# Layer 1's values by whole tiles of tokens, and four residual sums moved to TensorE, in a four-layer graph network on one core

## The chip, the cores and the metric

The kernel runs on one core of a Trainium2 chip. The metric is device time in microseconds (us), from the first to the last work of one execution; lower is better. The core has five engines that run side by side: TensorE (PE in the profile, with its weight loads as PEld), VectorE (DVE), ScalarE (ACT), GpSimd (POOL) and SyncE (SP), which issues the DMAs. In this kernel TensorE writes its results to PSUM, and VectorE and ScalarE bring them from there to SBUF.

## The reference

The input x has 128 graphs of 64 nodes with 256 features, all in FP32, and one 64 x 64 weighted adjacency matrix that all graphs share. Four layers follow, each with a residual and a layer norm around it:

```
x = layernorm(x + gnn0(x))   # A_hat x -> 512 -> batch norm, relu -> 256 -> batch norm
x = layernorm(x + gnn1(x))   # Chebyshev step, 4-head masked attention, MLP
x = layernorm(x + gnn2(x))   # two graph convolutions, then LSTMs over windows of 1..4 nodes
x = layernorm(x + gnn3(x))   # graph attention
```

Two places matter here. Layer 0 ends with a batch norm of its output over all tokens, whose scale and shift are known only when all tokens have been seen; then comes `x + out` and its layer norm. In layer 1 the attention needs queries, keys and values of the same tokens:

```
q, k, v = x1 @ Wq, x1 @ Wk, x1 @ Wv        # 4 heads of 64
o = softmax(mask(q k^T / 8)) v             # within each graph of 64 nodes
```

## The kernel before

The 8192 tokens are cut into 16 blocks of 512 (`TB`), which is 8 graphs. A block is held in SBUF either token-major (`tm`: 128 tokens in the partitions, four tiles of 256 features, `NT` = 4) or feature-major (`fm`: 128 features in the partitions, two chunks of 512 tokens). One such buffer is 128 x 1024 FP32. A token tile of 128 holds two graphs, one in each half of the partitions (`halves`).

Buffers come from two stocks. `PS` has four PSUM tiles of 128 x 1024; `mem` has SBUF tiles of the same shape. A step takes a tile, and the step that empties it gives it back.

The order of instructions on the engines is written by a planner, `flow`, while the program is built. Each task (one block of one layer, one LSTM unit, one load) is a generator. Before each group of instructions it yields `step(engine, us, ...)`: the engine, the planned duration, how many PSUM and SBUF tiles it takes, whether later steps of the task wait for it, and a label `tbl` that stands for an activation table on ScalarE or for the way TensorE's array is divided. A change of that label on TensorE is charged 0.1 us. At each turn `flow` takes the step that can begin soonest, after adding a margin that is multiplied by a pseudo-random factor; the numbers in `DRAWS`, one for each 50 us of planned time, choose these factors. So `DRAWS` decides the order of everything from the end of layer 0 on, but adds no work. Each engine executes its list in order and waits at semaphores for its inputs.

Where the plan leaves TensorE without work, `keep_awake` issues filler products of the identity (L142). Their number comes from the planned gap less 0.4 us, divided by 0.86 us.

Layer 0 runs as `first_block` and `second_block` for the 16 blocks; then `bn_coeffs` gives the batch norm's scale `sc2` and shift `sh2`. After that, one call of `flow` plans the end of layer 0 and layers 1 to 3 together. Its streams are the ends of layer 0 and the blocks of layer 1 (`seq`, up to six at a time), the graph convolutions of layer 2 (`gcn_block`), its LSTM units and the blocks of layer 3 (`last_block`).

`end_block(i)` ends layer 0 for one block. It loads x again from HBM (L771), applies scale and shift on ScalarE (L774, feature-major), transposes to token-major with 8 transposes of 128 x 128 (`to_tm`, L376), and adds x on VectorE out of PSUM (L782, one instruction of 128 x 1024). Block 0 (`NORMED`) is also normalised there; for the others `block` begins with that layer norm. A layer norm takes statistics on VectorE (L302 to L304), a power on GpSimd (L325), a small product on VectorE (L328) and four activations on ScalarE (L331). The blocks are not ended in their own order:

```
ends = (0, 1, 12, 13, 14, 15, 2, 3, 8, 9, 10, 11, 4, 5, 6, 7)
at_end = {0: 4, 1: 4, 2: 8, 3: 10, 4: 14, 5: 16}
```

so blocks 0, 1, 12 and 13 are ended before layer 1 begins block 0, and 14, 15, 2 and 3 before it begins block 2.

`block(i)` is layer 1 for one block: the norm, an aggregation with the graph's matrix in quarters of the array (L358), a product with Wc by whole token tiles (`mm_tm`, L394), an addition and a norm, the transposes to feature-major (`to_fm`, L370), the products with Wq and Wk (`mm_fm`, L382), the values (L846), the scores in quarters of the array (L872), the softmax, transposes of its result (L905), the product with the values in quarters (L919), Wo by `mm_tm`, and the MLP.

The values are computed graph by graph. For each of the 8 graphs and each half r of the heads, the stationary operand is 64 tokens of x1 (64 columns) and the moving one 128 columns of Wv; half r of the heads goes to half r of the PSUM partitions. So two products run in the two column halves of the array, and the PSUM tile has the layout that L919 wants: a whole-tile copy on ScalarE (L856) brings it to SBUF.

Of the kernel before, what the change touches and what calls it, by code (L numbers as in the profile page):

```python
# [11 lines left out]
ALU = mybir.AluOpType  # L12
# [3 lines left out]
P = 128  # L16
B, N, D = 128, 64, 256
NBLK = 16
TB = 512
NT = 4  # L20
# [8 lines left out]
LAG, LAG_T = 0.06, 0.2  # L29
MARGIN = {"T": 0.5, "V": 0.5, "S": 0.5}  # L30
STRETCH = 50.0
DRAWS = [119, 456, 684, 0, 152, 590, 97, 0, 0, 316, 775, 750, 291, 668, 396, 690, 972, 316, 700, 299, 810, 345, 289, 861, 902, 463, 567, 883, 455, 277, 848, 910, 108, 288, 531, 607, 103, 756, 415, 205, 829, 978, 419, 437, 870, 596, 976, 248, 270, 919]


@with_exitstack
def kernel(ctx: ExitStack, tc: tile.TileContext, a: dict, out: bass.AP):
    nc = tc.nc
    V, S, G, T = nc.vector, nc.scalar, nc.gpsimd, nc.tensor
# [11 lines left out]
    def tm(s):  # L50

        return s.rearrange("p (t d) -> p t d", t=NT)

    def fm(s):

        return s.rearrange("p (c k) -> p c k", c=2)
# [60 lines left out]
    def mark(*key):  # L117
        done[key] = Clock.end
# [7 lines left out]
    def step(e, us, ps=0, sl=0, waits=True, at=None, tbl=None):  # L126

        return (e, us, ps, sl, waits, at, tbl)
# [9 lines left out]
    def flow(streams, margin, start=0.0):  # L144
# [8 lines left out]
        def drawn(k, t):  # L153

            j = int(t / STRETCH)
            d = DRAWS[j] if j < len(DRAWS) else 0
            return (k * 7919 + j * 104729 + d * 1299709) * 2654435761 % 4294967296 / 2147483648 if d else 1.0
# [84 lines left out]
    def ctile(shape, name, pool=cp):  # L242
        return pool.tile(shape, F32, tag=name, name=name)
# [4 lines left out]
    Xs = [Xp[i // 2][:, i % 2, :] for i in range(NBLK)]  # L248
# [3 lines left out]
    H = [fm(s) for s in Hs]  # L252
# [3 lines left out]
    PS = Stock([ctile([P, NT * D], f"ps{j}", psp) for j in range(4)])  # L256
    mem = Stock([ctile([P, NT * D], f"t{j}", big) for j in range(TEMPS)])
# [15 lines left out]
    halves = slice(0, N), slice(N, P)  # L273
    for s in range(2):
        h = halves[s]
# [8 lines left out]
    ident = ctile([P, P], "ident")  # L284
# [34 lines left out]
    def ln_steps_act(y):  # L319

        n = y.shape[1]
        yield step("V", 0.3 + 0.53 * n)
        mv, rs = stats(y)
        yield step("G", 1.0)
        G.tensor_tensor(rs, rs, neghalf[:, :n], ALU.pow)  # L325
        yield step("V", 0.2, tbl="m")
        nm = sm.tile([P, n], F32, tag="ln_nm", name="ln_nm")
        V.scalar_tensor_tensor(nm, mv[:, :, 0], -1.0, rs, ALU.mult, ALU.mult)  # L328
        yield step("S", 0.1 + 0.5 * n)
        for t in range(n):  # L330
            S.activation(  # L331
                y[:, t, :], y[:, t, :], AF.Identity, scale=rs[:, t : t + 1], bias=nm[:, t : t + 1]
            )
# [38 lines left out]
    def to_tm(ps, yT):  # L372

        for t in range(ps.shape[1]):
            for c in range(2):
                T.transpose(ps[:, t, c * P : (c + 1) * P], yT[:, c, t * P : (t + 1) * P], ident)  # L376
# [13 lines left out]
    def mm_tm(ps, yT, w, nk):  # L390

        for t in range(NT):
            for k in range(nk):
                T.matmul(  # L394
                    ps[:, t, :],
                    yT[:, k, t * P : (t + 1) * P],
                    w[:, k, :],
                    start=(k == 0),
                    stop=(k == nk - 1),
                )  # L400
# [22 lines left out]
    with c0:  # L423
# [310 lines left out]
        Wc, Wq, Wk, Wv = (WA[:, j, :].rearrange("p (k m) -> p k m", k=2) for j in range(4))  # L734
# [24 lines left out]
    sc2, sh2, _ = bn["bn2"]  # L759

    Wv_par = Wv.rearrange("p k (u r e) -> p k r u e", u=2, r=2)

    NORMED = range(1)

    def end_block(i):
        x = X[i]
        yield step("Q", 6.0, sl=1)
        xin = mem.take()  # L770
        nc.sync.dma_start(tm(mem[xin]), x_blk[i])  # L771
        for c in range(2):
            yield step("S", 0.7)
            S.activation(  # L774
                H[i][:, c, :], H[i][:, c, :], AF.Identity, scale=sc2[:, c : c + 1], bias=sh2[:, c : c + 1]
            )
        yield step("T", 0.9, ps=1)
        ps = PS.take()
        to_tm(tm(PS[ps]), H[i])
        mark("h", i)  # L780
        yield step("V", 1.25, ps=-1)
        V.tensor_tensor(x, tm(PS[ps]), tm(mem[xin]), ALU.add)  # L782
        PS.give(ps)
        mem.give(xin)
        if i in NORMED:
            yield from ln_steps_act(x)
        mark("end", i)

    def block(i):
        x = X[i]  # L790
        mark("begun", i)
        if i not in NORMED:
            yield from ln_steps_act(x)
        yield step("T", 0.98, ps=1, sl=1, tbl="quarter")
        ps = PS.take()
# [6 lines left out]
        ps = PS.take()  # L802
# [14 lines left out]
        ps = PS.take()  # L817
        s_x1 = mem.take()
        to_fm(fm(PS[ps]), y)
        yield step("S", 1.05, ps=-1)  # L820
        x1T = fm(mem[s_x1])
# [3 lines left out]
        for w in (Wq, Wk):  # L825
            yield step("T", 3.45, ps=1, sl=1)
            ps = PS.take()
# [8 lines left out]
        qT, kT = fm(mem[qk[0]]), fm(mem[qk[1]])  # L836


        yield step("T", 3.6, ps=1, sl=1, tbl="columns")
        ps = PS.take()  # L840
        s_v = mem.take()
        pv = PS[ps].rearrange("p (b u e) -> p b u e", b=8, u=2)
        for b in range(8):
            for r in range(2):
                for k in range(2):
                    T.matmul(  # L846
                        pv[r * N : (r + 1) * N, b, :, :],
                        x1T[:, k, b * N : (b + 1) * N],
                        Wv_par[:, k, r, :, :],
                        start=(k == 0),  # L850
                        stop=(k == 1),
                    )
        mem.give(s_x1)
        yield step("S", 1.05, ps=-1, waits=False)
        v = mem[s_v].rearrange("p (b u e) -> p b u e", b=8, u=2)
        S.copy(mem[s_v], PS[ps])  # L856
        PS.give(ps)

        yield step("G", 2.4, waits=False, tbl="m")
# [4 lines left out]
        ps = PS.take()  # L864
        s_e = mem.take()
        pq = PS[ps].rearrange("p (r g m) -> p r g m", r=2, g=8)
        for t in range(NT):
            for u in range(2):
                for s in range(2):
                    b = 2 * t + s  # L870
                    for r in range(2):
# [4 lines left out]
                            start=True,  # L876
                            stop=True,
# [4 lines left out]
        e = mem[s_e].rearrange("p (g r m) -> p g r m", g=8, r=2)  # L882
# [19 lines left out]
        ps = PS.take()  # L902
# [9 lines left out]
        ps = PS.take()  # L912
        s_o = mem.take()
        po = fm(PS[ps])
        for b in range(8):
            t, s = b // 2, b % 2
            for u in range(2):
                for r in range(2):
# [4 lines left out]
                        start=True,  # L923
                        stop=True,
# [7 lines left out]
        ps = PS.take()  # L932
# [9 lines left out]
        ps = PS.take()  # L942
# [13 lines left out]
        for hf in range(2):  # L956
            yield step("T", 3.45, ps=1, sl=1)
            ps = PS.take()
# [14 lines left out]
        ps = PS.take()  # L973
        for t in range(NT):
            for k in range(4):
# [4 lines left out]
                    start=(k == 0),  # L980
                    stop=(k == 3),
# [487 lines left out]
    def sum_weights(p, sums):  # L1469
# [18 lines left out]
        for k in range(2):  # L1488
            i0, i1, h0, h1 = (w[:, k, :, c, :] for w in (ih, hh) for c in range(2))
            s1, s2, s3, s4 = (gates(sums[2 * i + k]) for i in range(4))  # L1490
            for dst, y, z, op in (
# [8 lines left out]
                else:  # L1500
                    for g in range(4):
                        V.tensor_tensor(S4[k][g], y[:, g], z[:, g], op)
        WS[p] = {
            "A11": block(ih, 0), "A12": block(hh, 0), "A22": block(hh, 1),
            "S1": whole(S1), "S2": whole(S2), "S3": whole(S3), "S4": whole(S4),
        }
# [136 lines left out]
    for i in blocks:  # L1643
        while n < at_end.get(i, NBLK):
            j = ends[n]
            seq.append((None, lambda j=j: end_block(j), 1))
            n += 1
        seq.append((lambda i=i: ready(("end", i)), lambda i=i: block(i), 5))
# [79 lines left out]
    def last_of(i, *part):  # L1728
# [17 lines left out]
        start=done["bn2", 0],  # L1746
# [49 lines left out]
```

## Time and profile before

| | |
|---|---|
| median of three runs | 2317.06 us (2316.89 to 2318.54) |
| the profiled execution's own time | 2318.26 us |
| its span, first to last instruction | 2316.5 us |
| mean granted TensorE clock | 0.997 |
| TensorE busy, filler included | 2270.1 us, 98% of the span |
| VectorE, ScalarE, GpSimd busy | 1332.9, 1176.1, 437.1 us (58%, 51%, 19%) |
| DMA moved | 57.90 MB, mean 25 GB/s |

Layer 0 lasts to about 250 us. The ends of layer 0 (L376, L782) lie between 257 and 426 us, the values of layer 1 (L846) between 294 and 1100 us, and layer 3's blocks in the last part.

A row of the timeline has the start, the duration, the engine and line, the operation with output and input by the program's names (buffer numbers left out), the shape and the number of instructions merged; in brackets stands idle time before it and what ended it. An FP32 product stands as two records, a transpose as one. Consecutive products overlap in the array, so the durations of single ones add up to more than the time that passes: the distance from one start to the next tells what a group costs. A row of busy time by stretches has the stretch, its length, the busy time of each engine with its instructions, the granted clock, the share of DMA and its GB/s.

### The profile page before, as it was taken

How to read it: one execution, taken by the hardware profiler on the slowest of the kernel's cores; microseconds unless marked ns; L12 is line 12 of the kernel's file. 1: busy time of each engine (PE TensorE's matmuls, PEld its weight loads, DVE VectorE, ACT ScalarE, POOL GpSimd, SP SyncE). 2: the span in 40 equal slices, each digit the busy share in tenths (PEclk: the TensorE clock that was granted, in tenths of full speed). 3: DMA queues.
4: the chain of work that ended last, by engine and by line, in shares of the span. 5: the costliest groups of instructions: out<-in, count | busy, mean ns of one | idle time of the engine just before them, and what ended most of it. 6: DMA issues, size and time to landing. Idle time of an engine off the chain costs nothing. (4 is left out here: it accounts for less than half of the span.)

```text
span 2316.5 us, 40592 instructions
## 1 busy us (share of the span) xinstructions
PE 2270.1 (98%) x16974; PEld 1757.4 (76%) x16974; DVE 1332.9 (58%) x2869; ACT 1176.1 (51%) x2265; POOL 437.1 (19%) x323
## 2 busy tenths in 40 slices
PE   8999999999999999999999999999999999999997
PEld 5558667666666767567667888999999889888884
DVE  5557776767565668437444444454445655664577
ACT  2257556555554545544544343444434644654576
POOL 0012133232322235113220001001100110111012
PEclk9999999999999999999999999999999999999999
DMA  6100411000000000000100000000001000001111
GB/s 173 47 1 1 138 38 33 10 11 10 10 10 10 11 10 19 28 2 28 37 28 19 1 1 1 19 1 1 1 1 37 1 10 28 19 19 37 37 56 55
DMA packets 42632, 57.90 MB, mean 25 GB/s; under 512 B 6224, under 2 KB 35536, under 8 KB 42448
## 3 DMA queue, kind: packets, MB, share of 16 engines
q1 hardware_dynamic: 41344, 54.22, 7.1%
q8 instruction: 133, 2.18, 0.4%
q10 hardware_dynamic: 1104, 1.08, 0.1%
q14 instruction: 51, 0.42, 0.1%
HBM read 38.52 MB, written 16.78 MB: 24 GB/s over the span
## 5 line engine op out<-in xcount | busy, mean ns | idle before, releaser
L325 POOL TENSOR_TENSOR ln_rs<-ln_rs,neghalf 128x4 f32<-128x4 f32 (+1 forms) x104 | 111.8, 1075 | 722.5 <-DVE ln_rs L304 573.0
L1185 PE MATMUL ps<-x,x 128*128 128x256 f32 x832 | 204.5, 379 | 0.0
L1185 PE MATMUL ps<-t,x 128*128 128x256 f32 x736 | 179.0, 380 | 0.8 <-DVE t L1244 0.8
L1081 ACT ACTIVATE x<-ps,bih 128x512 f32<-128x512 f32 (+5 forms) x185 | 95.5, 552 | 150.4 <-PE ps L1113 97.7
L1185 PEld LDWEIGHTS ps<-x,x 128*128 128x128 f32 x832 | 156.0, 190 | 18.7
L1185 PEld LDWEIGHTS ps<-t,x 128*128 128x128 f32 x736 | 138.2, 190 | 20.3 <-DVE t L1244 1.2
L1081 ACT ACTIVATE t<-ps,bih 128x512 f32<-128x512 f32 (+5 forms) x151 | 79.5, 563 | 127.2 <-PE ps L1113 85.0
L331 ACT ACTIVATE x<-x,ln_nm,ln_rs 128x256 f32<-128x256 f32 x212 | 110.2, 593 | 43.8 <-DVE ln_nm L328 43.3
L382 PE MATMUL ps<-t,W1T 128*128 128x512 f32 x256 | 115.3, 595 | 0.0
L1081 ACT ACTIVATE x<-x,bih 128x512 f32<-128x512 f32 (+5 forms) x142 | 72.1, 559 | 44.2 <-DVE x L1251 44.2
L303 DVE BATCH_NORM_AGGREGATE ln_mv<-ln_st 128x2 f32<-128x6 f32 x448 | 81.6, 182 | 15.3
L302 DVE BATCH_NORM_STATS2 ln_st<-x 128x6 f32<-128x256 f32 x224 | 89.7, 401 | 0.3
L1113 PE MATMUL ps<-h,wL 128*128 128x192 f32 (+2 forms) x456 | 89.7, 351 | 0.0
L1113 PE MATMUL ps<-h,x 128*128 128x256 f32 x384 | 86.8, 380 | 0.0
L1113 PE MATMUL ps<-t,wL 128*128 128x512 f32 x192 | 83.9, 593 | 1.2 <-ACT t L909 1.2
L1113 PEld LDWEIGHTS ps<-h,wL 128*128 128x128 f32 x456 | 70.0, 190 | 17.4 <-issue 16.7
L382 PEld LDWEIGHTS ps<-t,W1T 128*128 128x128 f32 x256 | 46.4, 190 | 47.5 <-issue 47.3
L1113 PEld LDWEIGHTS ps<-h,x 128*128 128x128 f32 x384 | 72.8, 190 | 10.4 <-issue 0.5
L1244 DVE COPY x<-ps 128x256 f32<-128x256 f32 (+2 forms) x71 | 26.7, 377 | 86.6 <-PE ps L1185 86.2
L1251 DVE TENSOR_TENSOR x<-ps,x 128x512 f32<-128x512 f32 (+2 forms) x71 | 42.4, 598 | 51.0 <-PE ps L1185 41.0
L331 ACT ACTIVATE t<-t,ln_nm,ln_rs 128x256 f32<-128x256 f32 x104 | 54.1, 592 | 32.1 <-DVE ln_nm L328 32.1
L1113 PEld LDWEIGHTS ps<-t,wL 128*128 128x128 f32 x192 | 36.3, 190 | 44.7 <-issue 42.8
(715 smaller groups left out, 5408.6 us busy)
## 6 DMA issues: line engine op xcount, KB each, us to landing
t<-in_x_dram SPq DMA_DIRECT2D x24, 512.0 KB, 5.5
xd<-x SPq DMA_DIRECT2D x16, 512.0 KB, 2.7
h<-in_x_dram SPq DMA_DIRECT2D x7, 512.0 KB, 4.0
x<-xd SPq DMA_DIRECT2D x6, 512.0 KB, 3.4
out_dram<-x SPq DMA_DIRECT2D x6, 512.0 KB, 2.9
wL<-in_L_gnn_Wih_dram SPq DMA_DIRECT2D x2, 1024.0 KB, 5.0
x<-in_L_gnn_Whh_dram SPq DMA_DIRECT2D x2, 1024.0 KB, 5.2
t<-xd SPq DMA_DIRECT2D x4, 512.0 KB, 4.3
```

Of the source, the lines that this page charges most:

```text
L302: V.bn_stats(st[:, t, :], y[:, t, :])
L303: V.bn_aggr(mv[:, t, :], st[:, t, :])
L325: G.tensor_tensor(rs, rs, neghalf[:, :n], ALU.pow)
L331: S.activation(y[:, t, :], y[:, t, :], AF.Identity, scale=rs[:, t : t + 1], bias=nm[:, t : t + 1])
L382: T.matmul(ps[:, c, :], w[:, k, (off + c) * P : (off + c + 1) * P], yT[:, k, :], start=(k == 0), stop=(k == nk - 1),)
L1081: S.activation(dst, z, AF.Tanh, bias=bl[:, p - 1, 2 * g + c : 2 * g + c + 1], scale=(1.0 if g == 2 else 0.5) * (1.0 if p == 1 else 0.5),)
L1113: T.matmul(spread(fm(PS[ps])[:, j, :n], q), WL[p][0][:, k, m], x_of(0, q)[:, k], start=(k == 0), stop=(k == 1),)
L1185: T.matmul(dst, WS[p][name](k, g), y[:, k], start=first and k == 0, stop=k == 1, skip_group_check=not first)
L1244: V.tensor_copy(y[:, 1, :], v[:, 0, :])
L1251: V.tensor_tensor(y[:, 0:2, :], v[:, 2:4, :], y[:, 0:2, :], ALU.add)
```

## The change

Three things change.

The values use whole token tiles. Instead of 32 products with 64 stationary columns there are 8 with 128: `mm_tm` with Wv in its stored layout, four token tiles by two chunks of features. The result has both graphs of a token tile in the two partition halves and all heads side by side, so it is parted on the way out: four ScalarE copies, one for each graph s of a token tile and each half r of the heads, each of 64 partitions and 512 elements. For s different from r a copy moves from one half of the partitions to the other. The rearranged view `Wv_par` goes.

Blocks 12 to 15 get their sum from TensorE. For these, x is multiplied by the identity into PSUM (4 products of 256 columns), and the 8 transposes become plain products against the identity that add to it. ScalarE copies the sum out, in place of VectorE's addition. The planned duration of the TensorE step is 2.65 us instead of 0.9.

`DRAWS` has new numbers, so the order from the end of layer 0 on is another one.

```diff
-DRAWS = [119, 456, 684, 0, 152, 590, 97, 0, 0, 316, ...]
+DRAWS = [555, 824, 612, 0, 95, 823, 924, 783, 0, 77, ...]
...
-    Wv_par = Wv.rearrange("p k (u r e) -> p k r u e", u=2, r=2)
...
+    SUM_BY_T = (12,13,14,15)
...
-        yield step("T", 0.9, ps=1)
-        ps = PS.take()
-        to_tm(tm(PS[ps]), H[i])
-        mark("h", i)
-        yield step("V", 1.25, ps=-1)
-        V.tensor_tensor(x, tm(PS[ps]), tm(mem[xin]), ALU.add)
+        yield step("T", 2.65 if i in SUM_BY_T else 0.9, ps=1)
+        ps = PS.take()
+        if i in SUM_BY_T:
+            for t in range(NT):
+                T.matmul(tm(PS[ps])[:, t, :], ident, tm(mem[xin])[:, t, :], start=True, stop=True)
+                for c in range(2):
+                    T.matmul(
+                        tm(PS[ps])[:, t, c * P : (c + 1) * P],
+                        H[i][:, c, t * P : (t + 1) * P],
+                        ident,
+                        start=False,
+                        stop=True,
+                        skip_group_check=True,
+                    )
+            mark("h", i)
+            yield step("S", 1.05, ps=-1)
+            S.copy(Xs[i], PS[ps])
+        else:
+            to_tm(tm(PS[ps]), H[i])
+            mark("h", i)
+            yield step("V", 1.25, ps=-1)
+            V.tensor_tensor(x, tm(PS[ps]), tm(mem[xin]), ALU.add)
...
-        yield step("T", 3.6, ps=1, sl=1, tbl="columns")
+        yield step("T", 3.45, ps=1, sl=1)
         ps = PS.take()
         s_v = mem.take()
-        pv = PS[ps].rearrange("p (b u e) -> p b u e", b=8, u=2)
-        for b in range(8):
+        mm_tm(tm(PS[ps]), x1T, Wv, 2)
+        mem.give(s_x1)
+        pv = PS[ps].rearrange("p (t u r e) -> p t u r e", t=NT, u=2, r=2)
+        v = mem[s_v].rearrange("p (b u e) -> p b u e", b=8, u=2)
+        yield step("S", 2.4, ps=-1, waits=False)
+        for s in range(2):
             for r in range(2):
-                for k in range(2):
-                    T.matmul(
-                        pv[r * N : (r + 1) * N, b, :, :],
-                        x1T[:, k, b * N : (b + 1) * N],
-                        Wv_par[:, k, r, :, :],
-                        start=(k == 0),
-                        stop=(k == 1),
-                    )
-        mem.give(s_x1)
-        yield step("S", 1.05, ps=-1, waits=False)
-        v = mem[s_v].rearrange("p (b u e) -> p b u e", b=8, u=2)
-        S.copy(mem[s_v], PS[ps])
+                S.copy(v[halves[r], s::2, :, :], pv[halves[s], :, :, r, :])
         PS.give(ps)
```

More of the change, by code (lines that the diff above doesn't have):

```diff
@@ L31 @@
 STRETCH = 50.0
-DRAWS = [119, 456, 684, 0, 152, 590, 97, 0, 0, 316, 775, 750, 291, 668, 396, 690, 972, 316, 700, 299, 810, 345, 289, 861, 902, 463, 567, 883, 455, 277, 848, 910, 108, 288, 531, 607, 103, 756, 415, 205, 829, 978, 419, 437, 870, 596, 976, 248, 270, 919]
+DRAWS = [555, 824, 612, 0, 95, 823, 924, 783, 0, 77, 0, 664, 0, 363, 656, 902, 351, 574, 489, 0, 99, 684, 176, 923, 880, 530, 427, 46, 867, 911, 330, 952, 468, 0, 995, 634, 121, 751, 0, 0, 274, 611, 895, 832, 143, 47, 41, 113, 989, 558]
 @with_exitstack
```

## The prediction

> **What bounds the kernel now.** I read the engines' totals first, then busy time by stretches, then single stretches of the timeline.
>
> ```profile
> PE 2270.1 (98%) x16974; PEld 1757.4 (76%) x16974; DVE 1332.9 (58%) x2869; ACT 1176.1 (51%) x2265; POOL 437.1 (19%) x323
> ```
>
> TensorE has work 98% of the span; nothing else passes 58%. But some of its work is filler (keep_awake, L142). Busy time in four stretches (length, then PE, PE weight loads, DVE, ACT, POOL):
>
> ```profile
> 250.00:300.00 50.00, 47.13 (x363) 30.79 (x362) 38.99 (x88) 29.44 (x45) 10.74 (x12) 1.00 0.34 110
> 300.00:1100.00 800.00, 793.41 (x7775) 539.53 (x7773) 512.47 (x1042) 425.11 (x603) 242.63 (x140) 1.00 0.05 16
> 1100.00:2200.00 1100.00, 1088.86 (x6355) 951.47 (x6354) 546.28 (x1141) 523.09 (x1194) 134.99 (x107) 1.00 0.05 16
> 2200.00:2316.50 116.50, 99.84 (x692) 76.38 (x691) 82.93 (x306) 80.60 (x222) 24.12 (x33) 0.95 0.17 55
> ```
>
> From 300 to 2200 us TensorE is idle 6.6 + 11.1 us: there its own work is the path, and a microsecond of it removed is a microsecond saved. From 250 to 300, between layers 0 and 1, it is not: 2.9 us idle, and of the 47.1 busy much is filler (the rows of L142 in this part):
>
> ```profile
> 250.14 7.03 PE L142 MATMUL ps<-ident 128*128 128x512 f32 x16
> 257.00 2.02 PE L376 MATMUL ps<-ident,h 128*128 128x128 f32 x17
> 259.52 1.86 PE L376 MATMUL ps<-ident,h 128*128 128x128 f32 x15 [0.50 <-ACT h L774]
> 261.21 5.32 PE L142 MATMUL ps<-ident 128*128 128x512 f32 x12
> ...
> 280.96 2.74 PE L142 MATMUL ps<-ident 128*128 128x512 f32 x6
> 284.44 1.06 PE L370 MATMUL ps<-ident,t 128*128 128x128 f32 x8 [0.74 <-DVE t L814]
> 285.34 1.02 PE L142 MATMUL ps<-ident 128*128 128x512 f32 x2
> ```
>
> With one more of 1.13 us, filler is 17.2 us, so TensorE lacks work for 20.1 of these 50 us. The path here runs through the norm of blocks 0 and 1:
>
> ```profile
> 262.60 0.17 DVE L304 TENSOR_SCALAR ln_rs<-ln_mv 128x4 f32<-128x4 f32 x1
> 262.68 2.36 DVE L782 TENSOR_TENSOR x<-ps,t 128x1024 f32<-128x1024 f32 x2
> 264.95 0.15 DVE L328 SCALAR_TENSOR_TENSOR ln_nm<-ln_mv,ln_rs 128x4 f32<-128x4 f32 x1
> ```
>
> By the order of `ends`, the two additions at 262.68 are those of blocks 12 and 13. GpSimd's power for block 0 ended at 263.93, but L328 ran only after them, and block 1's statistics began after it.
>
> **What the Trainium skill says.** "TensorEngine Tiling (Array Packing)", Key Properties: changing the tiling mode drains TensorE. This trace agrees, as 0.10 us at a change (below). "TensorE: Matmul & The Clock Gate", Terms, gives FP32 a transpose mode said to be four times faster. Here eight transposes take 0.87 us from start to next start and a plain product of the same columns twice that; I use the trace. The same page, Why this matters, wants no TensorE idle gap over some 3 us; the trace's mean granted clock is 0.997, and sums that take filler's place leave no such gap.
>
> **Part 1, values by whole tiles.** Per block, 32 products of 64 stationary columns become 8 of 128, as in L394. I measure from start to next start, since the durations overlap.
>
> ```profile
> 616.48 3.62 PE L394 MATMUL ps<-Wg,h 128*128 128x256 f32 x16
> 619.93 1.04 PE L370 MATMUL ps<-ident,h 128*128 128x128 f32 x8
> 620.90 3.77 PE L846 MATMUL ps<-wA,t 128*64 128x128 f32 x64
> 624.60 1.16 PE L358 MATMUL ps<-bdAT,h 64*64 64x64 f32 x64
> ```
>
> L394 between full-array neighbours takes 619.93 - 616.48 = 3.45 us; L846 takes 3.70 in all 16 blocks where it can be read so. The change of mode adds: the transposes before L846 take 0.97, elsewhere 0.87, and a full-array group after it about 0.08 more (3.53 against 3.44 for L382). Six of the 16 have full-array neighbours on both sides: 0.10 + 3.70 + 0.08 - 3.45 = 0.43 each. Ten have a quarter-array group on one side, where one change remains: about 0.24 each. Sum 6 x 0.43 + 10 x 0.24 = **5.0 us less**, all between 294 and 1100 us. Other neighbours in the new order give 4 (all 0.25) to 6.9 (all 0.43).
>
> ACT pays. One copy L856 of 128x1024 took 1.01 us; now four of 64 partitions by 512. The nearest row, a 128x512 copy from PSUM (L1576), took 0.585, with some 0.1 overlap: 4 x 0.5 = 2.0, so +1.0 per block, 16 us in all, beside an ACT at 53% busy in 300 to 1100. The cover is TensorE working on other blocks: the values are needed only at L919, after scores, softmax and L905. Queued behind the copies are other blocks' evictions, and one of four PSUM tiles is held 1 us longer. PE's listed waits in 300 to 1100 sum to 6.5 us, on ACT 3.3, so I take 0; bounds: 0, because a longer copy cannot speed anything, to 16 x 0.25 = 4 if a quarter of each delay surfaces.
>
> **Part 2, four sums on TensorE.** Each of blocks 12 to 15 had 8 transposes, 0.87 us by start to start. Now 4 products of 256 columns (half of L394's group, 1.72) and 8 of 128. Plain products against the identity issue two records each: L1029's two calls stand as x4 and take 294.54 - 294.00 = 0.54 with a mode change, so 0.22 each; 8 make 1.73. Together 3.45, **2.58 more each, 10.3 in all**. The plan books 2.65 - 0.9 = 1.75, so 3.3 of the 10.3 is unplanned.
>
> Where does it lie? The trace shows 12 and 13 between 257 and 261, beside 12.3 us of filler: 5.2 extra, covered. Blocks 14 and 15 stand at 274, ahead of 3.8 us of filler and about 1 us idle: 5.2 extra, nearly covered. Filler is counted by planned times, so unplanned work stays behind it. I put 1.5 us on the path; bounds 0 (all in gaps) to 10.3 (all in dense work).
>
> DVE loses 4 x 1.22 us, ACT gains 4 x 1.01. Without the pair at 262.68, L328 of block 0 could run at 263.95 instead of 264.95 and block 1's statistics 2.3 us earlier. ACT waited 4.96 us before 265.14, which holds the copies for 12 and 13. The next wait is the same chain in both blocks, then DVE: from 276 to 299 it is almost never idle, and blocks 14 and 15's additions stand in that stretch. So the dense part starts 1 to 2.4 us earlier; I take **1.5 less**. Bounds 0 (ACT's copies displace what DVE gave back) to 4.9 (all four additions on the path).
>
> **Part 3, the order.** DRAWS shifts when each step is preferred; no engine work is added, but idle and mode changes move. What can be won is TensorE's idle and filler after 300: 6.6 + 11.1 + 16.7 idle and 6.7 filler, 41 us. SP's loads and stores follow their tasks, so each queue's order shifts with it. No trace of before prices a different order: I take 0, with 8 less (a fifth of the 41 saved) to 10 more (a quarter added). A gain and a loss are both possible.
>
> **Sum.** -5.0 + 0 + 1.5 - 1.5 + 0 = -5.0 us on the profiled execution, 2318.26 us with a span of 2316.5. The median is 2317.06, 1.2 below it; the difference carries over: **2312.0 us**. A measurement of this kernel tells some 0.2%, 4.6 us, from no change: faster means below 2312.4, slower above 2321.7.
>
> **The rivals.**
>
> Evictions surface: ACT's four copies hold PSUM tiles and stand ahead of other copies, and the unplanned 3.3 us lands whole. For: PE's longest ACT wait after 300 is 1.2 us, on L909, a copy. Against: these waits are few. 2 us of copies and 1.8 us more of sums: 2315.8, no measurable change.
>
> The new order loses at the end (the slower one). The last 116.5 us hold 16.7 us idle and 6.7 filler; there the chain alternates between small steps of last_block on four engines. If the order lengthens it by half of that, 12 us, the time is 2324. It decides once more than 9.6 us is lost, since 5.0 is saved. Against: nothing in the end's steps changes. The four sums landing wholly in dense work would do nearly the same, -5.0 - 1.5 + 10.3 = +3.8, 2321, just short of it.
>
> The new order gains: 8 us of idle saved makes 2304.
>
> The change doesn't do what it says: the values in new surroundings pay mode changes anyway, saving 16 x 0.24 = 3.8: 2313.2.
>
> **Chances and range.** The sum as argued 0.45 (own range 2309 to 2315, with most of it under the bound), values at 3.8 only 0.08, evictions 0.20, order or sums losing 0.18, order gaining 0.09. Faster by over 0.2%: 0.50; within: 0.32; slower: 0.18. Range 2303 to 2323: down to the order's gain, up to nearly the whole loss at the end.
>
> **What would show it.** No 128*64 row remains; the values stand as 16 records of 128x256 at 3.45 us from start to start, with four ACT copies of about 0.5 us. A sum takes 3.4 to 3.5 us; 2.65 would show the second record free. Filler in 250 to 300 falls from 17.2 to about 8 us and the dense part begins by 299. The prediction is wrong if idle plus filler after 300 differs from 41 by over 5, if the sums stand after 300, or if PE's waits for ACT in 300 to 1100 exceed 6 us.

## The result and the profile after

The changed kernel takes 2320.26 us (median of 20 runs, 2317.68 to 2321.87) against 2317.02 for the kernel before (20 runs, 2314.68 to 2319.98). The ratio is 1.0013, with a 95% interval of [1.0007, 1.0019]: 3.0 us slower, [1.6, 4.4], where 5 us faster was forecast. That is within the 0.2% called no change, but on the other side.

First the page's totals, then busy time by stretches of the changed kernel (columns as before: stretch, length, PE, weight loads, DVE, ACT, POOL).

```profile
PE 2274.9 (98%) x16268; PEld 1756.9 (76%) x16268; DVE 1341.6 (58%) x2865; ACT 1199.1 (52%) x2315; POOL 436.1 (19%) x323
```

```profile
250.00:300.00 50.00, 49.59 (x362) 36.81 (x362) 31.50 (x87) 33.26 (x51) 9.54 (x12) 1.00 0.38 120
300.00:1100.00 800.00, 794.82 (x7122) 534.33 (x7121) 526.23 (x1020) 445.51 (x651) 245.46 (x139) 1.00 0.05 17
1100.00:2200.00 1100.00, 1084.56 (x6274) 946.13 (x6273) 551.16 (x1162) 522.10 (x1185) 133.71 (x108) 1.00 0.04 15
2200.00:2317.60 117.60, 105.88 (x725) 81.67 (x723) 82.67 (x307) 81.40 (x229) 23.05 (x32) 0.99 0.17 55
```

TensorE's idle time is 42.7 us (span less busy), before it was 46.4. L142's rows sum to 26.2 us, before to 26.8. What is left is TensorE's own work: 2317.6 - 42.7 - 26.2 = 2248.7 us, before 2243.3. The work grew by 5.4; the forecast's terms for it, -5.0 and +10.3, make 5.3. The gap between layers 0 and 1 took in 9.5 us of it: idle and filler there fell from 20.1 to 10.6. But idle in 1100 to 2200 rose from 11.1 to 15.4, and idle and filler after 300 together from 41 to 45.4. The two profiled spans differ by only 1.1 us, where the medians differ by 3; part of that is a scatter in the first 60 us, which is taken apart below.

Where the gap's time went is seen on TensorE, from the filler after layer 0 to the queries and keys of block 0 (L382):

```profile
250.95 7.03 PE L142 MATMUL ps<-ident 128*128 128x512 f32 x16
...
266.89 1.02 PE L142 MATMUL ps<-ident 128*128 128x512 f32 x2
267.85 1.16 PE L358 MATMUL ps<-LnT,x 64*64 64x64 f32 x64
...
281.96 0.59 PE L781 MATMUL ps<-t,ident 128*128 128x256 f32 x2
...
285.47 1.91 PE L376 MATMUL ps<-ident,h 128*128 128x128 f32 x16
287.21 1.04 PE L370 MATMUL ps<-ident,t 128*128 128x128 f32 x8
288.09 1.02 PE L142 MATMUL ps<-ident 128*128 128x512 f32 x2
289.41 7.13 PE L382 MATMUL ps<-t,wA 128*128 128x512 f32 x16 [0.30 <-ACT t L838]
```

L781 and L783 are the sums. The last one runs from 281.96 to 285.47, 3.5 us, as forecast. Behind it stand 16 transposes of other blocks, and only then block 0's (L370, 287.21), whose input was ready at 285.46 (end of L830 on DVE). From the filler's start to L382 it is 38.5 us; before it was 286.60 - 250.14 = 36.5. On ACT the copy of the third sum, L793, stands ahead of block 0's second norm:

```profile
278.70 1.01 ACT L793 COPY x<-ps 128x1024 f32<-128x1024 f32 x1 [0.80 <-PE ps L783]
279.61 2.07 ACT L331 ACTIVATE t<-t,ln_nm,ln_rs 128x256 f32<-128x256 f32 x4
```

L331 could have run from 278.87, when L328 ended on DVE. Its place in the queue made it 0.7 us later. In this trace that did not reach TensorE: block 0's result was ready at 285.46, and its transposes stood in TensorE's queue until 287.21.

One statement above needs correcting: DRAWS is also used when layer 0 is planned, so the order within layer 0 changed too, from about 70 us on. A product at about 60 us stands at the same place of both orders. Before:

```profile
60.75 3.60 PE L382 MATMUL ps<-t,W1T 128*128 128x512 f32 x8
```

The changed kernel, with waits of TensorE in layer 0 that before doesn't have:

```profile
59.12 3.60 PE L382 MATMUL ps<-t,W1T 128*128 128x512 f32 x8
...
94.58 0.38 PE L527 MATMUL ps<-ed,ones 128*128 128x1 f32 x2 [0.36 <-DVE ed L524]
118.56 0.91 PE L358 MATMUL ps<-AhT,t 64*64 64x64 f32 x43 [0.75 <-issue]
...
220.07 1.13 PE L659 MATMUL ps<-h,W2T 128*128 128x256 f32 x4 [0.18 <-ACT x L677]
241.57 1.13 PE L659 MATMUL ps<-h,W2T 128*128 128x256 f32 x4 [0.51 <-ACT x L677]
```

From this product to the filler that ends layer 0 it is 189.4 us in all four traces that keep the old order in full (before, values_only, values_straight, sums_only). It is 191.6 to 191.9 us in all eight that keep the new one (the changed kernel and the seven experiments made from it with its DRAWS). So the new order costs 2.2 to 2.5 us in layer 0. The scatter lies ahead of it: the product itself began between 59.1 and 61.9 us, whatever the order. The pair of traces then splits like this:

| part of the profiled execution | before, us | changed, us | difference, us |
|---|---|---|---|
| up to that product | 60.75 | 59.12 | -1.6 |
| from there to the filler after layer 0 | 189.39 | 191.83 | +2.4 |
| from the filler to the queries and keys (L382) | 36.46 | 38.46 | +2.0 |
| from there to the end | 2029.90 | 2028.19 | -1.7 |

Without the first row it is 2.7 us, near the 3.0 of the medians. The last row holds what the values save and what the order costs there, which the experiments part.

### The profile page after: what moved, and what is told of

Same layout as the page of the kernel before. It is cut to its first block, busy times and chain, and to the rows that moved or that the text cites. A ratio compares the mean times of both kernels' runs of the same rounds, so it can differ in the third digit from the quotient of the medians.

```text
span 2317.6 us, 39251 instructions
## 1 busy us (share of the span) xinstructions
PE 2274.9 (98%) x16268; PEld 1756.9 (76%) x16268; DVE 1341.6 (58%) x2865; ACT 1199.1 (52%) x2315; POOL 436.1 (19%) x323
## 4 chain that ended last, share of the span: by engine, by line
PE 93%; DVE 4%; ACT 2%; issue 1%; DMA 0%; POOL 0%; ACTq 0%; POOLq 0%; DVEq 0%
PE ps L1195 28%; PE ps L382 16%; PE ps L1123 15%; PE ps L394 10%; PE ps L986 4%; PE ps L659 4%; PE ps L358 3%; PE ps L1574 2%; PE ps L1331 2%; PE ps L370 2%; PE ps L1333 2%; PE ps L376 1%; PE ps L929 1%; PE ps L882 1%; PE ps L142 1%
## 5 line engine op out<-in xcount | busy, mean ns | idle before, releaser
L1195 PE MATMUL ps<-x,x 128*128 128x256 f32 x896 | 220.5, 380 | 0.3 <-DVE x L1263 0.3
L1195 PEld LDWEIGHTS ps<-x,x 128*128 128x128 f32 x896 | 167.2, 190 | 22.3 <-issue 1.3
L1091 ACT ACTIVATE t<-ps,bih 128x512 f32<-128x512 f32 (+5 forms) x174 | 91.1, 559 | 144.4 <-PE ps L1123 90.5
L1091 ACT ACTIVATE x<-ps,bih 128x512 f32<-128x512 f32 (+5 forms) x167 | 87.5, 557 | 145.0 <-PE ps L1123 107.0
L1195 PE MATMUL ps<-t,x 128*128 128x256 f32 x608 | 149.1, 379 | 0.0
L331 ACT ACTIVATE x<-x,ln_nm,ln_rs 128x256 f32<-128x256 f32 x224 | 116.3, 592 | 33.2 <-DVE ln_nm L328 32.8
L1195 PEld LDWEIGHTS ps<-t,x 128*128 128x128 f32 x608 | 114.1, 190 | 15.0 <-issue 0.5
L382 PE MATMUL ps<-t,W1T 128*128 128x512 f32 x256 | 115.1, 595 | 0.0
L1091 ACT ACTIVATE t<-t,bih 128x512 f32<-128x512 f32 (+2 forms) x120 | 60.3, 552 | 53.7 <-DVE t L1261 52.6
L382 PEld LDWEIGHTS ps<-t,W1T 128*128 128x128 f32 x256 | 46.5, 190 | 47.9 <-issue 47.8
L1091 ACT ACTIVATE x<-x,bih 128x256 f32<-128x256 f32 (+5 forms) x130 | 66.0, 560 | 30.7 <-DVE x L1261 30.6
L1123 PE MATMUL ps<-x,wL 128*128 128x512 f32 x168 | 73.3, 593 | 1.2 <-ACT x L1420 1.2
L331 ACT ACTIVATE t<-t,ln_nm,ln_rs 128x256 f32<-128x256 f32 x116 | 60.2, 591 | 22.7 <-DVE ln_nm L328 22.6
L1123 PEld LDWEIGHTS ps<-t,wL 128*128 128x128 f32 x192 | 36.4, 190 | 43.7 <-issue 43.3
L1123 PE MATMUL ps<-h,wL 128*128 128x144 f32 (+2 forms) x408 | 68.8, 323 | 0.0
```

What stands on the lines that cost most here:

```text
L331: S.activation(y[:, t, :], y[:, t, :], AF.Identity, scale=rs[:, t : t + 1], bias=nm[:, t : t + 1])
L382: T.matmul(ps[:, c, :], w[:, k, (off + c) * P : (off + c + 1) * P], yT[:, k, :], start=(k == 0), stop=(k == nk - 1),)
L1091: S.activation(dst, z, AF.Tanh, bias=bl[:, p - 1, 2 * g + c : 2 * g + c + 1], scale=(1.0 if g == 2 else 0.5) * (1.0 if p == 1 else 0.5),)
L1123: T.matmul(spread(fm(PS[ps])[:, j, :n], q), WL[p][0][:, k, m], x_of(0, q)[:, k], start=(k == 0), stop=(k == 1),)
L1195: T.matmul(dst, WS[p][name](k, g), y[:, k], start=first and k == 0, stop=k == 1, skip_group_check=not first)
```

## The experiments

Two things make them sharp. The planner's order depends only on the figures in the steps and on DRAWS, so a kernel can keep one order to the instruction and change what a step does. And the plan's own end, the last time that `flow` reaches while the program is built, can be set beside the measured time. It is a plan, not a measurement: 2312.7 us for the kernel before, 2311.9 for the changed one.

Differences below are ratios of the runs times 2317, with their intervals. The theories: **A**, engine work adds up and the new order cost the time; **B**, the longer copies on ScalarE eat the saving; **C**, the sums cost it. Added as the runs came in: **A'**, the saving counts only in an order planned with it; **D**, the new plan is no shorter than the old one in effect, and what it doesn't book is added; **E**, the overrun is absorbed and the order is worse late; **F**, the order is neutral.

### One part at a time

Values alone, in the old order (the planned figures stay 3.6 and 1.05):

```diff
-        (32 products, pv[r * N : (r + 1) * N, b] <- x1T, Wv_par)
+        mm_tm(tm(PS[ps]), x1T, Wv, 2)
...
-        S.copy(mem[s_v], PS[ps])
+        (the four copies of the change)
```

> The kernel before with its own order of steps kept, and only the values changed: 8 whole-tile products and four copies. Theory A (engine work adds up; the new order is what cost time): 4 to 6 us faster than before, since TensorE's dense part loses 5.0 us, about 2312. Rival B (the four ScalarE copies, 2.35 us for a block instead of 1.01, give the saving back): within 1.5 us of before. Theory C (the four sums cost the time): as A, 5 us faster.

Measured: -1.2 us [-3.0, +0.9]. The same with one copy:

```diff
-        (the four copies of the change)
+        S.copy(mem[s_v], PS[ps])
```

> As values_only, but the whole tile is copied out with one copy, as before, so the heads are not parted and the output is not the reference's; it isolates TensorE's share. Theory A: 5 us faster than before, and within 1 us of values_only. Rival B: 5 us faster, and at least 3 us faster than values_only. Theory C: as A.

Measured: -2.3 us [-4.2, -0.5]. A's number came in neither run. B's came for values_only, but B also had the single copy at least 3 us faster than the four; it is 1.1 us faster, which isn't separated from zero. TensorE's work did fall, from 2243.3 to 2237.0 us in values_only (1.7 us of this is a stretch at a lower clock, 0.83 from 790 to 800 us, that only the profile of before had). But idle in 300 to 1100 rose from 6.6 to 9.3. What TensorE waits for in layer 1 of values_only (waiter, what it waited for, sum, times, longest; this kernel's lines after the edit are seven lower than before):

```profile
PE ps L382 <- ACT t L822: 2.7, 2, 1.5
PE ps L358 <- ACT x L1366: 1.5, 1, 1.5
PE ps L370 <- DVE t L814: 1.4, 1, 1.4
PE ps L370 <- DVE ln_nm L328: 1.4, 1, 1.4
```

The wait for L822 was 1.1 before; those for L1366 and L814 were not there. My reading is A': an order made for a slower TensorE step brings the next steps too early for their inputs. These waits alone don't show it; the pairs of runs further below test it.

The sums alone, in the old order:

```diff
+            by_t: the change's products; S.copy(Xs[i], PS[ps]) in place of V.tensor_tensor
+            owed[0] += 2.58        # keep_awake issues that much less filler
```

> The kernel before with its own order of steps, the four sums on TensorE and copied out by ScalarE, and the filler after them shortened by 2.58 us a sum, as far as there is filler. Theory A: the 10.3 us of extra work take filler's place, 0 to 3 us slower than before. Rival B: 0 to 3 us slower as well. Theory C: 5 us slower or more, because the sums stand in the way of block 0's chain whatever the order is.

Measured: +16.2 us [13.2, 19.5], far above A and B and within C's open "5 us slower or more". Part is the setup's own. The copies stand where the additions stood, so on ACT the norm of block 0 queues behind a copy that waits for the second sum; and with less filler TensorE's clock fell, to 0.93 from 250 to 300 us. So this run says nothing on the sums in an order made for them.

The order alone, with the values and sums of before:

> The new order of steps (planned with the new figures and DRAWS), but with the values and all sums done as before; TensorE's filler stays as the new plan has it. Theory A: the new order alone is 4 to 8 us slower than before, since after 5.0 us of saving the changed kernel still was 3.2 us slower. Rival B and theory C: the order costs nothing, within 2 us of before (a little faster under C, since the new plan leaves gaps for sums that are not there).

Measured: +12.3 us [9.3, 15.1], more than A's 4 to 8. Here too the clock fell, because the sums that should fill the gap were missing (busy by stretches of order_only; the granted clock is the third number from the end):

```profile
250.00:300.00 50.00, 43.02 (x302) 28.20 (x304) 35.60 (x88) 29.02 (x46) 8.77 (x12) 0.93 0.40 127
```

At 0.93, 3.5 of the 50 us are lost.

### In the new order

The order again, with the gap kept full:

```diff
+            for _ in range(2):      # per sum, then the transposes and the addition as before
+                T.matmul(fm(PS[ps])[:, 0, :], ident, bc_mid(ident, 4), start=True, stop=True)
```

> The changed kernel's order alone: values and sums done as before, with two filler products of 0.86 us in place of each sum's extra booked time, so that the gap between the layers is as full as planned. Theory D (the new order is about as much longer as the planned savings are; values save 3.7 us in it, sums cost 4.2): 1.5 to 3.5 us slower than before, 2319.5. Rival F (the order itself is neutral, and values save less than they seem): within 1 us of before. The plan's own end, without any of its errors, was 2312.7 us for before and 2311.9 for the changed kernel.

Measured: +6.5 us [4.2, 9.0], more than theory D's figure; F falls. The gap isn't where it is lost: from the filler (251.71) to the queries and keys (288.06) it is 36.4 us, against 36.5 before. Layer 0 takes 191.6 us after the product at 60 us, 2.2 more than before, and from the queries to the end it is 3.7 us more. There TensorE is idle for 15.2 us in 1100 to 2200:

```profile
1100.00:2200.00 1100.00, 1084.80 (x6268) 947.56 (x6267) 552.32 (x1160) 521.11 (x1179) 132.73 (x106) 1.00 0.04 15
```

Then the values of the change with these fillers:

> The changed kernel with the four sums done as before (transposes, addition on VectorE), and two filler products of 0.86 us where each sum's extra booked time was, so that TensorE is neither idle nor late. Theory D: as sums_as_booked, within 1.5 us of before. Rival E: 2 to 4 us slower than before.

Measured: -1.2 us [-3.0, +0.9], as D says. And the sums of the change with the old values:

> The changed kernel in its own order, with only the values done as before (32 products of 64 columns, one copy). Theory A' (TensorE's saving of about 4 to 5 us counts in the new order, because it was planned there): 3 to 5 us slower than the changed kernel, 6 to 8 us slower than before. Rival B (the longer copies give most of it back, as they did in the old order): within 2 us of the changed kernel, 1 to 5 us slower than before.

Measured: +6.7 us [4.2, 9.0]. So in the new order the values save 7.7 us without the sums (6.5 to -1.2) and 3.7 with them (6.7 to 3.0); the sums cost 4.2 us with the new values and 0.2 with the old ones. The four runs' intervals are up to 2.5 us wide on a side; whether the two parts really interact is left open.

The sums shortened to what the plan books:

```diff
-                for c in range(2):
+                for c in range(1):
```

> The changed kernel, with four of the eight 128-column products of each sum left out (half of layer 0's result is then missing from four blocks), so that a sum takes about 2.6 us of TensorE, the 2.65 that its plan books, instead of 3.5. Theory D (the new plan is about as long as the old one, and the 0.8 us a sum that it does not book are added): 3 to 3.5 us faster than the changed kernel, so within 1 us of before. Rival E (the overrun is absorbed by gaps, and the new order is worse in layers 2 and 3): within 1 us of the changed kernel, 2 to 4 us slower than before.

Measured: -1.2 us [-3.0, +0.7], 4.2 below the changed kernel. E falls. On TensorE, this kernel's filler and L382:

```profile
253.28 7.03 PE L142 MATMUL ps<-ident 128*128 128x512 f32 x16
...
288.86 7.13 PE L382 MATMUL ps<-t,wA 128*128 128x512 f32 x16 [0.30 <-ACT t L838]
```

From one to the other it is 35.6 us instead of 38.5: of the overrun of 3.2 us, 2.9 was on the path there, by this pair of traces.

Does it act through the filler behind the sums?

```diff
+            owed[0] += 0.8          # per sum, taken off the next filler
```

> The changed kernel, with the filler behind the sums shortened by 0.8 us for each sum, which is what the sum overruns its plan by. If the filler behind the sums of blocks 12 and 13 is what delays block 0's aggregation at 267.85 us: 0.5 to 1.5 us faster than the changed kernel, 1.5 to 2.5 slower than before. If the overrun acts through the copies queued on ScalarE and the sums queued ahead of block 0's transposes instead: no difference from the changed kernel, 3 us slower than before.

Measured: +2.5 us [0.9, 3.9], 0.5 below the changed kernel, though filler in 250 to 300 fell from 10.2 to 7.0 us. The medians don't tell the two expectations apart. The trace says that the filler has a share: from the filler after layer 0 (253.54) to the queries and keys (291.14) it is 37.6 us, 0.9 less than in the changed kernel. Shorter sums win more there, 2.9 us in sums_as_booked, so most of the delay goes with the length of the sums and what queues behind them on TensorE. And the copies of the values:

> The changed kernel, with one whole-tile copy of the values (1.01 us instead of 2.35) in place of the four, so the heads are not parted and the output is not the reference's. If the longer copies cost time in the new order, where they are planned at 2.4 us: 1 us or more faster than the changed kernel. Theory D: no difference, within 1 us of the changed kernel, about 2320, since the order was made with that length and no TensorE wait of the changed kernel in layer 1 names them.

Measured: +3.0 us [1.4, 4.4], the changed kernel's time. In the order that plans them no cost of the four copies is seen, and B, which has them eat the saving, falls there; by the two intervals, a cost of up to some 2 us isn't excluded.

### The order fitted again

DRAWS was searched anew by changing one or two entries at a time and keeping what shortens the plan. First the whole change, its sums booked as long as they are:

```diff
-        yield step("T", 2.65 if i in SUM_BY_T else 0.9, ps=1)
+        yield step("T", 3.45 if i in SUM_BY_T else 0.9, ps=1)
```

> The change with its sums booked at 3.45 us instead of 2.65, and DRAWS fitted again for that: the planned end is 2310.8 us, against 2311.9 of the changed kernel (which lacks the 3.2 us) and 2312.7 of before. Theory D (the plan's end plus what it does not book sets the time): 1 to 3 us faster than before, about 2315. Rival E (the sums cost their 10 us wherever they are booked): 2 us or more slower than before.

Measured: 2315.41 us, -2.1 [-3.7, -0.7], as D says. The booking and the new search were changed together, so their shares in the 5.1 us are not told apart. Then the values alone, with their own figures:

```diff
+DRAWS = [370, 503, 149, 0, 0, 487, 247, 725, 0, 0, 0, 0, 461, 301, 0, 226, 788, 365, 382, 0, 760, 834, 0, 102, 0, 863, 875, 472, 870, 704, 0, 91, 940, 0, 231, 0, 428, 643, 319, 857, 258, 683, 567, 167, 197, 833, 91, 0, 0, 0]
...
+        yield step("T", 3.45, ps=1, sl=1)      # values of the change, copies booked at 2.4
```

> The values changed as in the change, the four sums left on VectorE, and DRAWS fitted again with the values' new figures: the planned end is 2309.0 us, against 2312.7 of before. Theory D: 3 to 4.5 us faster than before, about 2313. Rival B (the longer copies cost what they save): within 1 us of before.

Measured: 2311.73 us, ratio 0.9975 [0.9966, 0.9984], -5.8 us [-7.9, -3.7], more than D's 3 to 4.5. This version beats both kernels. Its busy time by stretches:

```profile
300.00:1100.00 800.00, 795.22 (x7131) 533.92 (x7130) 527.81 (x1028) 453.71 (x656) 251.90 (x143) 1.00 0.04 15
1100.00:2200.00 1100.00, 1089.54 (x6302) 956.61 (x6301) 555.11 (x1161) 521.50 (x1189) 128.60 (x105) 1.00 0.05 16
```

Idle is 4.8 and 10.5 us, below the changed kernel's 5.2 and 15.4: the work is less and the order no worse than before's.

Was it the fit or the values? The kernel before, only DRAWS fitted further:

> The kernel before, no step changed, DRAWS alone fitted further by the same kind of search as for refit_values: the planned end is 2311.3 us against 2312.7. If fitting longer is what made refit_values 5.8 us faster: 4 us or more faster than before. Theory D (the planned end moves the time, one for one): 0.5 to 2.5 us faster than before, about 2315.8, so that most of refit_values' gain needs the values' change.

Measured: -1.2 us [-3.2, +0.7]. And the order of refit_values with the old values:

> refit_values with its order kept and the values done as before (32 products, one copy). Theory A': 4 to 7 us slower than refit_values, 1 us faster to 1.5 us slower than before, as TensorE's saving counts in an order that was made with it. Rival F (values save under 2 us, the fit did the rest): within 2 us of refit_values.

Measured: -1.4 us [-3.2, +0.5], so the values are worth 4.4 us in this order (5.8 less 1.4). The three pairs of runs that price them in an order planned with them give 7.7, 3.7 and 4.4, 5.3 on average, against 1.2 (2.3 with one copy) in the old order. By itself only the first is clear of 1.2, given the intervals; the average is.

The plan's end beside the median of the same session (before had 2316.8 to 2317.3 in the sessions):

| kernel | plan's end, us | measured, us | difference |
|---|---|---|---|
| before | 2312.7 | 2317.3 | 4.6 |
| changed, as booked | 2311.9 | 2320.3 | 8.4 |
| changed, plus 4 x 0.8 | 2315.1 | 2320.3 | 5.2 |
| refit_booked | 2310.8 | 2315.4 | 4.6 |
| refit_before | 2311.3 | 2315.9 | 4.6 |
| refit_values | 2309.0 | 2311.7 | 2.7 |

With the unbooked 3.2 us put in, the plan's ends rank the five kernels rightly, but they don't price them: D's numbers for order_filled and refit_values missed, and the difference runs from 2.7 to 5.2. Layer 0 is a part that the plan has wrong. It ends at 256.61 us by the plan of the old order and at 256.35 by the plan of the new one, 0.3 earlier, where the traces have 2.2 to 2.5 more. The layer 0 of refit_booked takes as long as the changed kernel's (191.8 us after the product at 60 us), and yet its difference is 4.6, so other errors stand against this one.

## Why the prediction was wrong

**The order** is the step that failed first: "I take 0". By itself it was 6.5 us slower, inside the stated bound of 8 less to 10 more, but no zero. Its reason was that no engine work is added. But DRAWS, once fitted, is part of the kernel: a fit finds places for waits, and the two fits ended only 0.8 us apart by their own plans, 2312.7 and 2311.9. The loss shows in two places that the change doesn't touch. One is layer 0, 2.2 to 2.5 us, which the prediction left out because it took DRAWS to act only from the end of layer 0 on. The other is idle time of TensorE in 1100 to 2200: 14.9 to 16.0 us in the eight traces of the new order, 11.1 to 11.9 in the four of the old one. Together that is about 6 us. In layer 0 the fit could not see the loss, since its plan has none there; why it took the waits in 1100 to 2200 is not shown. The rival "the new order loses" had the right cause with the wrong place: the last 117 us lost nothing (11.7 us idle and 9.4 filler, before 16.7 and 6.7).

**The sums' overrun** was mis-sized: "I put 1.5 us on the path". Their price was right, 3.5 us against 3.45 forecast. The overrun of 3.2 us cost 2.9 in the gap and 4.2 in all, measured by sums_as_booked; the 1.3 in between lie within the noise. Cover was counted in filler, but filler stands where the plan puts it; an overrun first delays what is queued behind the sum, filler included.

**The earlier start** was wrong: "I take 1.5 less". L328 of block 0 did come a microsecond sooner after layer 0 (264.78 - 250.95 = 13.8 us after the filler's start; before 264.95 - 250.14 = 14.8), as argued. Then L358, which needs L331's end near 267.06, waited behind the sums and one filler to 267.85, and the microsecond was gone. The queries and keys of block 0 began 2.0 us later after layer 0, not 1.5 earlier.

**The values** were sized well: 5.0 us forecast; 3.7 and 7.7 in the new order, 4.4 in refit_values' order. The parts are as said: no 128*64 row is left, and the first block's values take 301.68 - 298.13 = 3.55 us with a change of mode behind them. What was wrong is "a microsecond of it removed is a microsecond saved": in the old order only 1.2 of 5.0 arrived [-0.9, 3.0]. The Trainium skill's "TensorEngine Tiling (Array Packing)", Key Properties, on the drain at a mode change, stands: that 3.55 is 3.45 plus 0.10.

**The copies** at 0 fit what was measured in the planned order, though one took 0.58 us where 0.5 was forecast (L866; four make 2.35):

```profile
L866 ACT COPY t<-ps x36: 561/580/586, 301.8 to 1085.3; 64x512 f32<-64x512 f32 x36
```

So the sum -5.0 + 0 + 1.5 - 1.5 + 0 reads by measurement, on one path through the runs: order +6.5, values -7.7, sums +4.2, together +3.0. On the other path, with the sums ahead of the values, it is +6.5, +0.2 and -3.7.

## What to carry to other kernels

Where an order is fitted, an edit and its fit are two changes: keep the order fixed to price the edit, compare the two fits' own ends before crediting either, and look for the order's cost in every stage that it plans, those included that the edit doesn't touch. Book a step at its real length, from the trace, since in an in-order queue an overrun lands on what stands behind it; filler in another place doesn't cover it. Saved work on the busiest engine may hardly count in an order planned without it (1.2 of 5.0 us here) and count once the order is made with it (5.3 on average).

## What the runs showed that was not expected

TensorE's clock reacts to small gaps here. In order_only two waits of 2.49 and 3.23 us lay in the gap between the layers, some 20 us apart. After each the granted clock was 0.66 over the next 5 us, which makes 0.93 over the 50 us, and the products L382 behind the second took 8.23 us instead of 7.13. The same order with the gap filled stayed at 1.00 and was 5.8 us faster (6.5 against 12.3).

The Trainium skill's "TensorE: Matmul & The Clock Gate", Why this matters for your kernels, sets the limit at gaps over some 3 us; these traces show drops after shorter ones. All five waits of TensorE of 2.49 to 3.31 us in the kept traces (the first 20 us and the last 15 left out) were followed by a lower clock within 5 us. Of the twelve of 1.79 to 2.19 us, five were; of the shorter ones down to 1.2 us, only one of 1.21 us was, 8 us behind one of 1.84. One of 1.81 us stands in before, where the clock was 0.66 over the next 5 us:

```profile
796.29 3.90 PE L394 MATMUL ps<-Wg,x 128*128 128x256 f32 x9 [1.81 <-DVE t L885]
```

What decides for the short ones is not shown.
